# Explicit hand-out of six PSUM banks, and additions of the projection moved ahead of a step's first eviction

## The chip, the cores and the metric

The kernel runs on one core of a Trainium2 chip. The core has a matrix engine (TensorE, PE in the profile; its weight loads have a row of their own, PEld), a vector engine (VectorE, DVE), a scalar engine (ScalarE, ACT), GpSimd (POOL) and a queue that only issues transfers (SyncE, SP). Each engine works through its own list of instructions in order and waits on semaphores for the others. Results of TensorE go to PSUM, whose banks hold 128 partitions of 512 float32 values each, and VectorE and ScalarE read them from there.

The metric is device time in microseconds (us) of the whole program, lower is better. The time before is the median of three runs, 3659.57 us (3655.64 to 3660.37).

## The reference, cut to what matters

`x` has 16 samples of 256 channels on a 64 by 64 grid, all in float32. Two residual layers follow each other:

```python
x = x + conv(_gn(x))         # layer 0: group norm, then a grouped 3x3 convolution whose kernels are
                             # rotated per sample and group by angles computed from the pooled sample
x = x + attention(_gn(x))    # layer 1: group norm, then linear attention with 8 heads,
                             # a 5x5 depthwise convolution of the values, and a projection
...
q = relu(q) + 1e-6 ; k = relu(k) + 1e-6          # both over softplus(scale)
q = q ** 3 ; k = k ** 3                          # and rescaled to their norms of before
z = 1.0 / (einsum('bic,bc->bi', q, k.sum(axis=1)) + 1e-6)
kv_state = einsum('bjc,bjd->bcd', k, v)
out = einsum('bic,bcd->bid', q, kv_state) * z[..., None]
out = out + depthwise5x5(v)
out = out @ Wproj.T + bproj
```

## The kernel before, in words

A sample's 4096 positions are taken in 16 pairs of 128. For each sample `b` there is a key phase (`key_step`, positions by the pair: key and value products, the powers, and the sum of key times value that is kept in PSUM), a short passage (`between`) and an attention phase (`attention_step`, called with `p` = 1 to 17). Inside the `tc.manual_schedule()` of the main loop the order of instructions on each engine is the order of the calls in the code, so the calls of `attention_step` are to be read as a list of work for each engine.

An attention step works on three pairs at once, each at another stage. On TensorE the order is: `turn(b, p-1)` transposes the queries (tile `pt`, L698), `query_products(b, p+1)` makes the next queries (`pq`, L683), `turn_back(b, p-2)` transposes the attention output (`po`, L734), `attend(b, p-1)` multiplies with the key-value sum (`pn`, L715, in two PSUM banks of its own), `project(b, p-2)` makes the projection (`py`, L744). `add_up(b, p-3)` on VectorE adds the projection of the pair before to `x` in place (L756, two instructions), and `store` sends a finished quarter of the sample out once in four steps.

Into six of a sample's steps the convolution of the next sample is woven. `convolve(b+1, u, part)` comes last on TensorE in steps 2, 3, 4 (`u` = 0) and 9, 10, 11 (`u` = 1), with the parts A, P and B; it fills four tiles `pc` at once (L405), one for each `q` from 0 to 3. They are emptied in the step after, by `evict` with `q` = 0 to 3, spread over that step. A part A is emptied by ScalarE alone (L432). A part P is read twice: ScalarE writes it negated to one half of the rows (L428), then VectorE adds it to the other half (L434). A part B is added by VectorE (L430). I call a step by the part that it empties: an A step (p = 3 and 10), a P step (4 and 11), a B step (5 and 12). All but the last sample have a next one, so there are 15 samples with two P steps each, 30 in all.

All of these tiles but `pn` and the key-value sum, that is `pk`, `pt`, `pq`, `po`, `py`, `pd`, the four `pc` and some small ones, come from one PSUM pool of six places, `ps`, under one tag, "bank". A tile is asked for by `bank(name)`; which of the six places it gets is left to the framework, which takes one that is free as the program is laid out and makes the first matmul into it wait until the last reader of the tile before it is done. With four `pc` and one `py` held over the end of a step, a step that empties a convolution begins with one place free.

The lines that matter:

```python
        if part:
            evict(b + 1, u, part, 0)        # L864
        if p >= 3:
            add_up(b, p - 3)                # L866
            store(b, p - 3)
        if p - 1 < NP:
            turn(b, p - 1)                  # L870: asks for pt
            turned(b, p - 1)
        if part:
            evict(b + 1, u, part, 1)
        if p < NP:
            cube(f[p])
        if p + 1 < NP:
            query_products(b, p + 1)        # L877: asks for pq
```

Of the kernel before, what the change touches and what calls it, by code (L numbers as in the profile page):

```python
# [9 lines left out]
F32 = mybir.dt.float32  # L10
# [3 lines left out]
PSUM = bass.MemoryType.PSUM  # L14

P = 128
# [5 lines left out]
CH = 512  # L22
# [2 lines left out]
ROWS = CH // W  # L25


STRIP = 2 * ROWS
PAIRS = ROWS
LATE, LEAD = 3, 2  # L30
# [33 lines left out]
def conv_attention(ctx: ExitStack, tc: tile.TileContext, x, consts, kw, b1, w2, b2, b2r,  # L64
# [4 lines left out]
    def pool(name, bufs, **kw):  # L69
        return ctx.enter_context(tc.tile_pool(name=name, bufs=bufs, **kw))  # L70
# [7 lines left out]
    sp = pool("stats", 2)  # L78
    wtp = pool("wt", 1)
    dcp = pool("scratch1", 1, space=bass.MemoryType.DRAM)  # L80
    ps = pool("ps", 6, space=PSUM)
    psk = pool("psk", 1, space=PSUM)

    def const(name, shape, src=None):
# [2 lines left out]
            nc.sync.dma_start(t, src)  # L87
        return t

    def bank(name):  # L90
        return ps.tile([P, CH], F32, tag="bank", name=name)

    def halves(a):
        return a.rearrange("(t p) n -> p t n", p=P)
# [90 lines left out]
    def gn_coefs(st, b, which):  # L185


        mv = sp.tile([P, 2, 2], F32, tag="mv", name=f"mv{which}_{b}")
        for t in range(2):
            nc.vector.bn_aggr(mv[:, t, :], st[:, t])  # L190
        yield
        mean, var = mv[:, :, 0], mv[:, :, 1]
        co = sp.tile([P, 5, 2], F32, tag=f"co{which}", name=f"co{which}_{b}")
        a, pooled, d, v, m = (co[:, k, :] for k in range(5))
        pm = bank(f"pm{which}_{b}")[:, 0:2]
        nc.tensor.matmul(pm, lhsT=g8, rhs=mean, start=True, stop=True)
        nc.vector.tensor_copy(m, pm)
        nc.vector.tensor_sub(d, mean, m)
        nc.vector.tensor_mul(v, d, d)
        nc.vector.tensor_add(v, v, var)  # L200
        yield
        pv = bank(f"pv{which}_{b}")[:, 0:2]
        nc.tensor.matmul(pv, lhsT=g8, rhs=v, start=True, stop=True)
        vs = sp.tile([P, 2], F32, tag="vs", name=f"vs{which}_{b}")
        nc.vector.tensor_scalar(vs, pv, EPS_GN, None, ALU.add)
        nc.gpsimd.tensor_tensor(a, vs, mhalf, ALU.pow)
        yield
        if which == 0:
            nc.vector.tensor_mul(pooled, d, a)
        return a, pooled, m  # L210
# [7 lines left out]
    def prepare(b):  # L218
# [13 lines left out]
                                 start=t == 0, stop=t == 1)  # L232
        h = sp.tile([HID, 2], F32, tag="h", name=f"h_{b}")
        nc.vector.tensor_add(h, ph, b1_t)
        nc.vector.tensor_scalar(h, h, 0.0, None, ALU.max)
        yield
        pa = bank(f"pa_{b}")[:, 0:2 + 2 * HD]
# [10 lines left out]
        nc.vector.tensor_add(z, pa[:, 0:2], b2_t)  # L248
        mod = r_mod
        nc.vector.tensor_add(mod, pmod, b2r_t)  # L250

        nc.scalar.activation(mod, mod, AF.Tanh, scale=0.5)
        cs = sp.tile([P, 3, 2], F32, tag="cs", name=f"cs_{b}")
# [5 lines left out]
        pe = bank(f"pedge_{b}")[:, 0:NH]  # L259
        nc.tensor.matmul(pe, lhsT=sel, rhs=gm.rearrange("p t j -> p (t j)"), start=True, stop=True)  # L260
        nc.vector.tensor_copy(edge, pe)
        state[b]["edge"] = edge
        nc.vector.tensor_scalar(mod, mod, 0.5, 0.5, ALU.mult, ALU.add)
        yield
# [59 lines left out]
        def shifts(t):  # L324


            pb = bank(f"pbias_{b}_{t}")[:, 0:3]
            for j in range(4):
                for dx in range(3):
                    nc.tensor.matmul(pb[ts(j, HD), dx:dx + 1], lhsT=sums[t][:, dx, :], rhs=gm[:, t, j:j + 1],  # L330
                                     start=True, stop=True, tile_position=(0, HD * j))
            nc.vector.tensor_copy(shift[:, t, 0:3], pb)
            nc.vector.tensor_reduce(shift[:, t, 3:4], shift[:, t, 0:3], AX.X, ALU.add)
            nc.vector.tensor_scalar(shift[:, t, 3:4], shift[:, t, 3:4], -1.0, None, ALU.mult)

# [83 lines left out]
    def evict(b, u, part, q):  # L419

        at, shift = (2 * u + q // 2, q % 2), state[b]["shift"][:, q % 2, 3:4]
        pc = state[b]["pc"][q].rearrange("p (r w) -> p r w", w=W)
        fresh = at not in state[b]["x"]
        if fresh:
            state[b]["x"][at] = xp.tile([P, 2 * CH], F32, tag="x", name=f"x_{b}_{at[0]}_{at[1]}")
        rows = rows_16(b, u, q)
        if part == "P":
            nc.scalar.activation(rows[:, 1], pc, AF.Identity, bias=shift, scale=-1.0)  # L428
        if part == "B":
            nc.vector.tensor_add(rows[:, 1], pc, rows[:, 1])  # L430
        elif fresh:
            nc.scalar.activation(rows[:, 0], pc, AF.Identity, bias=shift)  # L432
        else:
            nc.vector.tensor_add(rows[:, 0], pc, rows[:, 0])  # L434

    def settle(b, u, s, q):

# [28 lines left out]
    for name, src, bsrc in (("kv", wkv, brow[C:3 * C]), ("q", wq, brow[0:C])):  # L466
        n = src.shape[1]
# [27 lines left out]
    for (w, br), lo in zip(wl.values(), (0, 2 * C)):  # L495
# [3 lines left out]
        n = w.shape[2]  # L499
# [3 lines left out]
    pb = bank("pb")[:, 0:2]  # L503
    for co in range(2):
        for t in range(2):
            nc.tensor.matmul(pb[:, co:co + 1], lhsT=wp_t[:, t, ts(co, P)], rhs=dwb_t[:, t:t + 1],
                             start=t == 0, stop=t == 1)
    nc.vector.tensor_add(bp_t, bp_t, pb)


    vpad = [dcp.tile([BC, H + 4, NJ, C], F32, tag=f"vpad{n}", name=f"vpad{n}") for n in range(2)]
# [21 lines left out]
    def fold_shift(b, name):  # L533
        w, br = state[b][name]
        n = br.shape[1]
        pb = bank(f"pb{name}_{b}")
        for t in range(2):
            nc.tensor.matmul(pb[:, 0:n], lhsT=state[b]["gn1"][1][:, t:t + 1].to_broadcast([P, P]), rhs=w[:, t, :],
                             start=t == 0, stop=t == 1)
        nc.vector.tensor_sub(br, br, pb[:, 0:n])  # L540

    def norm1(b):
        a, _, m = yield from gn_coefs(state[b]["st1"], b, 1)
# [11 lines left out]
    def relu(r, pm, bias):  # L555

        nc.vector.tensor_add(pm, pm, bias)  # L557
        nc.vector.tensor_tensor(r, pm, eps_t.unsqueeze(1).to_broadcast(r.shape), ALU.max)
# [33 lines left out]
    def key_bias(b, n, j):  # L592
        _, br = state[b]["kv"]
        f = state[b]["k"][n]
        pm = f["pm"][j]
        relu(f["r"][:, j:j + 1, :], pm[:, 0:C].unsqueeze(1), br[:, 0:C].unsqueeze(1))
        nc.vector.tensor_add(vbuf[n % NV][:, j, 0:HD, :].rearrange("p c h -> p (c h)"), pm[:, C:2 * C], br[:, C:2 * C])

    def key_store(b, n):
        for j in range(2):  # L600
# [47 lines left out]
    def depthwise(b, half, c):  # L648


        if c == 0:
            state[b]["fm"] = fmp.tile([P, 16, C], F32, tag="fm", name=f"fm_{b}_{half}")
        fm = state[b]["fm"]
        vb = vh[0:KP].rearrange("p R (m j) (c h) -> p R m j c h", j=4, h=NH)
        pd = bank(f"pd_{b}_{half}_{c}").rearrange("p (k n) -> p k n", k=4)
        for k in range(4):
            for j in range(4):
                nc.tensor.matmul(  # L658
                    pd[ts(j, HD), k, :].rearrange("p (R m h) -> p R m h", R=4, m=4),
                    lhsT=band_t[:, c + k, :],  # L660
                    rhs=vb[:, :, :, j, c + k, :],
                    start=True, stop=True,
                    tile_position=(0, HD * j),
                )
        nc.scalar.copy(fm[:, :, c * NH:(c + 4) * NH].rearrange("p T (k h) -> p k T h", k=4),
                       pd.rearrange("p k (T h) -> p k T h", h=NH))


    def blocked(b, m):
# [19 lines left out]
    def query_bias(b, m):  # L689
        f = state[b]["f"][m]  # L690
        relu(f["r"], f["pq"], state[b]["q"][1].unsqueeze(1).to_broadcast([P, 2, C]))

    def turn(b, m):

# [6 lines left out]
    def turned(b, m):  # L701
        qT = op.tile([P, 2, 2, P], F32, tag="qT", name=f"qT_{b}_{m}", bufs=1)
        nc.scalar.copy(qT, state[b]["pt"])  # L703
        state[b]["qT"] = qT

    def attend(b, m):
# [22 lines left out]
    def turn_back(b, m):  # L729

        po = bank(f"po_{b}_{m}").rearrange("p (t j n) -> p t j n", t=2, j=2)
        for j in range(2):
            for t in range(2):
                nc.tensor.transpose(po[:, t, j, :], state[b]["o"][j][:, ts(t, P)], ident)  # L734
        oT = op.tile([P, 2, 2 * P], F32, tag="oT", name=f"oT_{b}_{m}", bufs=1)
        nc.scalar.copy(oT.rearrange("p t (j n) -> p t j n", j=2), po)  # L736
        state[b]["oT"] = oT

    def project(b, m):
# [12 lines left out]
    def add_up(b, m):  # L752
        i, R = divmod(m, 2)
        for co in range(2):
            xt = chunk(b, i, co).rearrange("p (y R n) -> p R y n", y=BR, R=2)[:, R]
            nc.vector.scalar_tensor_tensor(xt, state[b]["py"][:, co], bp_t[:, co:co + 1], xt, ALU.add, ALU.add)  # L756

    def store(b, m):
        I, R = divmod(m, 4)
        if R == 3:  # L760
            for t in range(2):
                nc.sync.dma_start(out[b, ts(t, P), ts(I, 2 * CH)], state[b]["x"].pop((I, t)))
# [89 lines left out]
    def attention_step(b, p, chain):  # L852
# [4 lines left out]
        f = state[b]["f"]  # L857
        n = p - NP - 2 + LEAD if more else -1
        u, part = PARTS.get(p - 1, (None, None)) if more else (None, None)
        v, s, early, late = SETTLES.get(p, (0, 0, (), ())) if more else (0, 0, (), ())  # L860
        if p - 1 < NP:
            ratio(f[p - 1], True)
            root(f[p - 1])
        if part:  # L864
            evict(b + 1, u, part, 0)
        if p >= 3:  # L866
            add_up(b, p - 3)
            store(b, p - 3)
        if p - 1 < NP:
            turn(b, p - 1)  # L870
            turned(b, p - 1)
# [13 lines left out]
        if n >= 0:  # L885
            k = state[b + 1]["k"]
# [179 lines left out]
```

## Time and profile before

| what | value |
|---|---|
| median of three runs | 3659.57 us |
| the profiled execution's own time | 3660.74 us |
| its span, from the first to the last instruction | 3659.0 us |
| mean granted TensorE clock | 0.994 of full speed |
| busy: VectorE, ScalarE, GpSimd | 2541.2, 2034.6 and 1980.4 us (69, 56 and 54% of the span) |
| projection added to x (L756) | 512 instructions, 474 ns median |
| part P added by VectorE (L434) | 120 instructions in the woven steps, 681 ns median |
| part P written by ScalarE, part A likewise (L428, L432) | 0.69 us each |
| part B and part A convolution (L405), start to start of the next `pt` | 6.51 and 6.46 us |

The profile is one execution. Its span is 1.7 us shorter than that execution's own time, which is 1.2 us above the median. A row of the timeline gives start and duration in us, engine, line, operation, and in brackets how long the engine was idle before it and which instruction ended that idle time. A row of the table of waits gives who waited, for whom, and then the sum in us, the number of times and the longest.

### The profile page before, as it was taken

The numbers are of one execution on the slowest core, as the hardware profiler recorded it, in microseconds if no ns is written. First come the engines' busy times: TensorE is split into PE (matmuls) and PEld (weight loads), VectorE is DVE, ScalarE is ACT, GpSimd is POOL, SyncE is SP. The second block draws the span as 40 slices with busy tenths as digits, with TensorE's granted clock in tenths as the row PEclk, the third lists the DMA queues.
The fourth block names the chain that finished last, engine by engine and source line by source line (L and its number), as shares of the span: only waits on it lengthen the run. The fifth ranks groups of instructions, "written<-read, shape, count | busy, mean of one in ns | idle before, by whom it ended". The sixth has DMA issues, their size and how long they took to land. (4 is left out here: it accounts for less than half of the span.)

```text
span 3659.0 us, 109568 instructions
## 1 busy us (share of the span) xinstructions
PE 3425.6 (94%) x43496; PEld 2563.6 (70%) x43496; DVE 2541.2 (69%) x6883; ACT 2034.6 (56%) x6501; POOL 1980.4 (54%) x2298
## 2 busy tenths in 40 slices
PE   2899999999999999999999999999999999999999
PEld 1467777776777767776677777777777677767778
DVE  4667768676686767767677686776866677676656
ACT  2365655647556465654656556475564646546565
POOL 4255555556555465554655555565554655546545
PEclk9899999999999999999999999999999999999999
DMA  4353552625436253452635526354362534525242
GB/s 134 110 180 106 161 159 86 197 87 184 140 115 190 83 189 111 150 172 72 203 106 161 158 87 193 91 185 139 113 191 84 186 114 148 168 77 181 78 145 99
DMA packets 191172, 505.90 MB, mean 138 GB/s; under 512 B 30741, under 2 KB 103959, under 8 KB 178372
## 3 DMA queue, kind: packets, MB, share of 16 engines
q1 hardware_dynamic: 190660, 498.89, 42.8%
q8 instruction: 344, 5.64, 0.6%
q14 instruction: 168, 1.38, 0.1%
HBM read 363.24 MB, written 135.53 MB: 136 GB/s over the span
## 5 line engine op out<-in xcount | busy, mean ns | idle before, releaser
L588 PE MATMUL pk<-wkv,x 128*128 128x512 f32 x2048 | 951.5, 611 | 0.0
L726 POOL TENSOR_TENSOR o<-o,fm 128x256 f32<-128x256 f32 x512 | 364.8, 733 | 918.9 <-DVE o L724 704.7
L588 PEld LDWEIGHTS pk<-wkv,x 128*128 128x128 f32 x2048 | 617.6, 310 | 213.6 <-issue 6.5
L683 PE MATMUL pq<-wq,xq 128*128 128x256 f32 x2048 | 492.2, 383 | 21.7 <-DVE x L434 11.5
L744 PE MATMUL py<-oT,wp 128*128 128x256 f32 x2048 | 505.7, 390 | 0.8 <-ACT oT L736 0.7
L564 ACT ACTIVATE r_k<-rk 128x256 f32<-128x256 f32 x1024 | 416.3, 407 | 152.9 <-POOL rk L567 92.6
L564 ACT ACTIVATE r_q<-rq 128x256 f32<-128x256 f32 x1024 | 413.5, 408 | 138.5 <-POOL rq L567 135.9
L683 PEld LDWEIGHTS pq<-wq,xq 128*128 128x128 f32 x2048 | 369.9, 191 | 72.1 <-DVE x L434 15.3
L736 ACT COPY oT<-po 128x512 f32<-128x512 f32 x256 | 150.1, 586 | 469.5 <-PE po L734 469.1
L744 PEld LDWEIGHTS py<-oT,wp 128*128 128x128 f32 x2048 | 369.2, 189 | 51.4 <-issue 3.6
L567 POOL TENSOR_TENSOR rk<-r_k,rk 128x512 f32<-128x512 f32 x256 | 327.0, 1277 | 96.7 <-ACT r_k L564 94.1
L576 POOL TENSOR_TENSOR s_k<-s_k,phalf 128x2 f32<-128x2 f32 x256 | 176.8, 691 | 356.9 <-DVE s_k L573 345.5
L557 DVE TENSOR_TENSOR pq<-pq,bq 128x512 f32<-128x512 f32 x256 | 177.4, 693 | 272.7 <-PE pq L683 230.6
L608 ACT ACTIVATE rk<-rk,s_k 128x256 f32<-128x256 f32 x512 | 231.4, 499 | 213.7 <-POOL s_k L576 213.7
L567 POOL TENSOR_TENSOR rq<-r_q,rq 128x512 f32<-128x512 f32 x256 | 327.2, 1278 | 0.0
L384 POOL TENSOR_TENSOR arena<-arena 128x512 f32<-128x512 f32 x244 | 303.8, 1279 | 7.1 <-PE pc_0B L405 3.7
L557 DVE TENSOR_TENSOR pk<-pk,bkv 128x256 f32<-128x256 f32 x512 | 218.0, 426 | 121.7 <-PE pk L588 119.9
L703 ACT COPY qT<-pt 128x512 f32<-128x512 f32 x256 | 148.7, 581 | 261.9 <-PE pt L698 260.2
L715 PE MATMUL pn<-kvx,qT 128*128 128x132 f32 x2048 | 274.0, 277 | 0.0
L576 POOL TENSOR_TENSOR s_q<-s_q,phalf 128x2 f32<-128x2 f32 x256 | 179.3, 700 | 144.1 <-DVE s_q L573 140.4
L715 PEld LDWEIGHTS pn<-kvx,qT 128*128 128x128 f32 x2048 | 250.5, 190 | 3.7 <-ACT qT L703 3.1
L658 PE MATMUL pd<-vh,band 107*32 107x128 f32 x8192 | 236.3, 274 | 6.5 <-issue 4.5
(161 smaller groups left out, 5974.1 us busy)
## 6 DMA issues: line engine op xcount, KB each, us to landing
vh<-vpad SPq DMA_DIRECT2D x256, 384.0 KB
vh<-vpad SPq DMA_DIRECT2D x256, 360.0 KB
vpad<-arena SPq DMA_DIRECT2D x512, 128.0 KB
out<-x SPq DMA_DIRECT2D x128, 512.0 KB
xs<-in_x SPq DMA_DIRECT2D x224, 256.0 KB
arena<-in_x SPq DMA_DIRECT2D x248, 144.0 KB
arena<-in_x SPq DMA_DIRECT2D x248, 136.0 KB
xs<-in_x SPq DMA_DIRECT2D x16, 512.0 KB
```

Source lines behind the costliest of these rows:

```text
L384: nc.gpsimd.tensor_add(s[:, j], g[:, j, odd:odd + STRIP:2], g[:, j, even:even + STRIP - 1:2])
L557: nc.vector.tensor_add(pm, pm, bias)
L564: nc.scalar.activation(f["r2"][:, j, :], f["r"][:, j, :], AF.Square, accum_out=f["s"][:, k, j:j + 1])
L567: nc.gpsimd.tensor_mul(f["r"], f["r2"], f["r"])
L576: nc.gpsimd.tensor_tensor(f["s"][:, 3, :], f["s"][:, 2, :], phalf, ALU.pow)
L588: nc.tensor.matmul(pm, lhsT=chunk(b, n // 2, t)[:, T % BC:CH:BC], rhs=w[:, t, :], start=t == 0, stop=t == 1)
L608: nc.scalar.mul(f["r"][:, j, :], f["r"][:, j, :], f["s"][:, 3, j:j + 1])
L658: nc.tensor.matmul(pd[ts(j, HD), k, :].rearrange("p (R m h) -> p R m h", R=4, m=4), lhsT=band_t[:, c + k, :], rhs=vb[:, :, :, j, c + k, :] ...
L683: nc.tensor.matmul(pq[:, j, :], lhsT=xq[:, t, ts(j, P)], rhs=w[:, t, :], start=t == 0, stop=t == 1)
L715: nc.tensor.matmul(pn[:, :, 4 * hh:4 * hh + 4], lhsT=qT[:, hh, j, :], rhs=kvx[:, hh], start=True, stop=True)
L726: nc.gpsimd.tensor_add(o, o, fm[:, 2 * (m % NCH) + j, :])
L744: nc.tensor.matmul(py[:, co].rearrange("p y (J c) -> p J y c", c=BC), lhsT=wp_t[:, t, ts(co, P)], rhs=oT[:, t, :].rearrange("p (J y c) -> ...
```

## The change

It does two things. The pool of six interchangeable places becomes six tags with one place each, `bank0` to `bank5`. A list `idle` in the code holds the names of the free ones; `bank(name)` takes the first of the list, and a new call `leave(name)`, put in the code behind the last reader of each tile, appends its place to the end. So the order of the calls in the code decides which place a tile gets. And in `attention_step` the lines `add_up` and `store` come before `evict(…, 0)` and no longer after it.

```diff
+BANKS = 6
...
-    ps = pool("ps", 6, space=PSUM)
+    ps = pool("ps", 1, space=PSUM)
...
+    idle, held = [f"bank{k}" for k in range(BANKS)], {}
+
     def bank(name):
-        return ps.tile([P, CH], F32, tag="bank", name=name)
+        held[name] = idle.pop(0)
+        return ps.tile([P, CH], F32, tag=held[name], name=name)
+
+    def leave(name):
+        idle.append(held.pop(name))
...
         else:
             nc.vector.tensor_add(rows[:, 0], pc, rows[:, 0])
+        leave(f"pc_{b}_{u}{part}_{q}")
...
         relu(f["r"], f["pq"], state[b]["q"][1].unsqueeze(1).to_broadcast([P, 2, C]))
+        leave(f"pq_{b}_{m}")
...
         nc.scalar.copy(qT, state[b]["pt"])
+        leave(f"pt_{b}_{m}")
...
         nc.scalar.copy(oT.rearrange("p t (j n) -> p t j n", j=2), po)
+        leave(f"po_{b}_{m}")
...
             nc.vector.scalar_tensor_tensor(xt, state[b]["py"][:, co], bp_t[:, co:co + 1], xt, ALU.add, ALU.add)
+        leave(f"py_{b}_{m}")
...
-        if part:
-            evict(b + 1, u, part, 0)
         if p >= 3:
             add_up(b, p - 3)
             store(b, p - 3)
+        if part:
+            evict(b + 1, u, part, 0)
         if p - 1 < NP:
             turn(b, p - 1)
             turned(b, p - 1)
```

The other tiles of the pool (`pk`, `pd` and the small ones of the norms and the rotation) get a `leave` behind their last reader in the same way. No instruction is added or removed.

More of the change, by code (lines that the diff above doesn't have):

```diff
@@ L197, in gn_coefs @@
         nc.vector.tensor_copy(m, pm)
+        leave(f"pm{which}_{b}")
         nc.vector.tensor_sub(d, mean, m)
@@ L205, in gn_coefs @@
         nc.vector.tensor_scalar(vs, pv, EPS_GN, None, ALU.add)
+        leave(f"pv{which}_{b}")
         nc.gpsimd.tensor_tensor(a, vs, mhalf, ALU.pow)
@@ L234, in prepare @@
         nc.vector.tensor_add(h, ph, b1_t)
+        leave(f"ph_{b}")
         nc.vector.tensor_scalar(h, h, 0.0, None, ALU.max)
@@ L250, in prepare @@
         nc.vector.tensor_add(mod, pmod, b2r_t)
+        leave(f"pa_{b}")
         nc.scalar.activation(mod, mod, AF.Tanh, scale=0.5)
@@ L261, in prepare @@
         nc.vector.tensor_copy(edge, pe)
+        leave(f"pedge_{b}")
         state[b]["edge"] = edge
@@ L332, in shifts @@
             nc.vector.tensor_copy(shift[:, t, 0:3], pb)
+            leave(f"pbias_{b}_{t}")
             nc.vector.tensor_reduce(shift[:, t, 3:4], shift[:, t, 0:3], AX.X, ALU.add)
@@ L508, in conv_attention @@
     nc.vector.tensor_add(bp_t, bp_t, pb)
+    leave("pb")
     vpad = [dcp.tile([BC, H + 4, NJ, C], F32, tag=f"vpad{n}", name=f"vpad{n}") for n in range(2)]
@@ L540, in fold_shift @@
         nc.vector.tensor_sub(br, br, pb[:, 0:n])
+        leave(f"pb{name}_{b}")
     def norm1(b):
@@ L597, in key_bias @@
         nc.vector.tensor_add(vbuf[n % NV][:, j, 0:HD, :].rearrange("p c h -> p (c h)"), pm[:, C:2 * C], br[:, C:2 * C])
+        leave(f"pk_{b}_{2 * n + j}")
     def key_store(b, n):
@@ L666, in depthwise @@
                        pd.rearrange("p k (T h) -> p k T h", h=NH))
+        leave(f"pd_{b}_{half}_{c}")
     def blocked(b, m):
```

## The prediction
> **What bounds the kernel now.** I read the page first, then the waits of TensorE, then the timeline of single steps. The page says that TensorE (PE) is nearly always busy:
>
> ```profile
> span 3659.0 us, 109568 instructions
> ...
> PE 3425.6 (94%) x43496; PEld 2563.6 (70%) x43496; DVE 2541.2 (69%) x6883; ACT 2034.6 (56%) x6501; POOL 1980.4 (54%) x2298
> ```
>
> That leaves 3659.0 - 3425.6 = 233 us of idle TensorE, the only time that a change of order can win. The table of waits, TensorE only, splits it. Of the rows that recur in every sample these matter:
>
> ```profile
> PE po L734 <- POOL o L726: 57.8, 148, 1.1
> ...
> PE pq L683 <- DVE x L434: 11.5, 16, 0.7
> PE pq L683 <- ACT qT L703: 10.2, 14, 0.7
> ```
>
> Large single waits (16.5, 16.0, 15.4, 14.7 us) lie before the main loop and stay. The first row is data: the transpose waits for the attention output. The other two are odd, since the query products `pq` need neither the convolution's rows (L434) nor the turned queries (L703). They can only wait for the place in PSUM. 16 + 14 = 30 is the number of P steps, and going through the timeline I find the wait in every P step and in no other. One P step in full:
>
> ```profile
> 993.15 0.69 ACT L428 ACTIVATE x<-pc_1P,shift 128x512 f32<-128x512 f32 x1 [2.41 <-PE pc_1P L405]
> 993.24 0.66 PE L698 MATMUL pt<-consts,rq 128*128 128x128 f32 x4
> 993.87 0.69 DVE L434 TENSOR_TENSOR x<-pc_1P,x 128x512 f32<-128x512 f32 x1 [1.83 <-ACT x L428]
> 993.99 0.59 ACT L703 COPY qT<-pt 128x512 f32<-128x512 f32 x1 [0.15 <-PE pt L698]
> 994.48 0.86 DVE L756 SCALAR_TENSOR_TENSOR x<-py,bp,x 128x256 f32<-128x256 f32 x2
> 994.62 1.99 PE L683 MATMUL pq<-wq,xq 128*128 128x256 f32 x8 [0.72 <-DVE x L434]
> 995.26 0.68 DVE L434 TENSOR_TENSOR x<-pc_1P,x 128x512 f32<-128x512 f32 x1
> 996.45 0.60 PE L734 MATMUL po<-consts,o 128*128 128x128 f32 x4
> 996.65 0.70 DVE L557 TENSOR_TENSOR pq<-pq,bq 128x512 f32<-128x512 f32 x1 [0.70 <-PE pq L683]
> ```
>
> `pt` ends at 993.90, `pq` starts at 994.62, just behind the end of the first L434 (993.87 + 0.69 = 994.56). That L434 is late because ScalarE reads the same bank first, and ScalarE had to wait for the convolution's end. VectorE idled 1.83 us before it, while the additions of the projection (L756), ready for a whole step, stood behind it in its queue. The A step just before shows the order without the wait:
>
> ```profile
> 984.46 0.66 PE L698 MATMUL pt<-consts,rq 128*128 128x128 f32 x4
> 984.95 1.89 PE L683 MATMUL pq<-wq,xq 128*128 128x256 f32 x8
> 986.47 0.57 PEld L734 LDWEIGHTS po<-consts,o 128*128 128x128 f32 x4
> 986.68 0.60 PE L734 MATMUL po<-consts,o 128*128 128x128 f32 x4
> ```
>
> From `pt` to `po` is 2.22 us there and 3.21 us in the P step.
>
> **The queue of places, by hand.** Call the one free place at a step's start X, the projection's Y, the convolution's c0 to c3. Before: evict 0 frees c0, then the addition frees Y, so longest-free first is X, c0, Y: `pt` takes X, `pq` takes c0, `po` takes Y. That the framework hands out this way is a reading, but it fits: taking the latest freed place, `pt` would have waited for L756 until 995.34, and it started at 993.24. The other row, L703, would mean that `pq` took X from `pt`; but in the P steps that I compared both releasers end within 0.03 us of each other, and in A steps `pq` starts before L703 does. After: X, Y, c0. `pt` takes X, `pq` takes Y, `po` takes c0. The next convolution takes c1, `pq`'s place, c2 and `po`'s place, by the same releases as before.
>
> **The change part by part.** *The additions first.* L756 (0.86 us for two) runs in VectorE's gap: its work before ends at 992.04 (L573, from 990.89, 1.15 us long), so they end near 992.9, before `pt` ends. Cost: nothing, covered by the 1.83 us of idle time; without that cover a P step would pay 0.86 us, 30 x 0.86 = 26 us. In B steps VectorE idles 1.41 us at the same point, and 0.83 us before L557 anyway, so nothing is won or lost there; in A steps evict 0 is ScalarE's, and VectorE's order doesn't change. No transfer changes its order on SP: an eviction issues none, and the store waits for the same L756.
>
> *The wait.* With Y free at 992.9, `pq` can follow `pt` at 0.49 us as in the A step. `po` then needs c0, free at 994.56; it would come at 993.24 + 2.22 = 995.46, so it doesn't wait. `pn` needs the turned queries of 994.58 and would come at 995.9. Per P step TensorE wins between 0.72 us (the idle time alone) and 3.21 - 2.22 = 0.99 us (start to start).
>
> *What is late next.* The B convolution at the step's end. Its third bank is c2, released by the L434 that starts at 999.62 and ends at 1000.29, 0.59 us behind the convolution's start at 999.70; the weight loads idle 0.45 us there, and the whole part takes 6.51 us against 6.46 for A, so that 0.05 us is lost today. VectorE's chain to this L434 runs from L557, which waited 0.70 us for `pq`. Now it is held by the second L434: ScalarE's second L428 ends at 994.47 + 0.69 = 995.16, so that L434 ends near 995.87, and L557 starts near 995.80 (engines overlap neighbours by 0.07) in place of 996.65: 0.85 us earlier, where the convolution is 0.99 us earlier. The bank comes 0.14 us later, relative to its matmuls. I take all of this as lost: 0.99 - 0.14 = 0.85 us per P step, the value inside the two bounds that the rows of the step give.
>
> *The place by tag.* The price in other steps is nothing where the first place of the list has long been left. I followed the list through a plain step (five free, four asked for, each left a step earlier), the key steps (one held at a time, six in turn), and the depthwise group of p = 9, the tightest: its sixth tile gets `pq`'s place, left at 970.81 by L558, and is due near 967.55 + 5 x 0.87 = 971.9. All have cover; the last has 1.1 us.
>
> *Sum.* 30 x 0.85 = 25.5 us; 3660.74 - 25.5 = 3635.2 against this execution, 3659.57 - 25.5 = 3634.1 against the median, which I predict. Bounds: 30 x 0.72 = 21.6 gives 3638.0, 30 x 0.99 = 29.7 gives 3629.9.
>
> **A rule weighed against it.** The rows first: in the P step the weight loads of `pq` begin only at 994.61, after 0.96 us without any. The Trainium skill, page "TensorE: Matmul & The Clock Gate", section "Architectural detail: the array is 16× 32×32, not 1× 128×128", says that the engine's queue can pull weight loads ahead of matmuls in flight. By that rule the loads would be done during the wait, only the matmul's 0.72 us would be lost, and the sum would be 21.6 us. By the rows, where load and matmul start together, it is the larger one.
>
> The page "Perfetto Trace Analysis", section "Identifying the Most-Contended Engine", calls matmul busy time no good measure of how close TensorE is to its limit. That speaks against taking the 94% for a bound; the sum above rests on starts of matmuls alone, and by the page it would be the same.
>
> **The rivals.** *The time goes to the next wait (no change).* If the L434 behind the B convolution's third bank kept its time, the bank would come 0.59 + 0.99 us after the start and give all back: 3659.6. For it: that wait exists (17 times 0.5 us on PEld for each half). Against: VectorE's chain there waits on `pq` itself. Chance 0.07. *It doesn't do what it says:* if places were handed out otherwise than I read, `pq` may have waited for something else that stays: 3659.6 again. Against: the list in the code is explicit now. 0.03.
>
> *Slower.* In the A steps of p = 10 the evictions of q = 0 and 1 ask for new tiles in SBUF, and the store now comes ahead of them. If they got the places that this very store is emptying, ScalarE would stand in evict 0 until the transfer has landed, with the turned queries behind it in its queue, `pn` behind those, and TensorE behind `pn`. The store is issued at 979.47, evict 0 is due at 983.97, and the transfers' share falls from 0.95 to 0.05 at 983.5, so it would cost about nothing. From 25.5 / 15 = 1.7 us per sample it eats the gain, from 2.2 us (another 7.3 / 15) it makes the kernel slower. With a landing 3 us late: 15 x 3 - 25.5 = +19.5, 3679. Chance 0.07.
>
> **How the numbers follow.** What a measurement of this kernel can tell from no change is about 0.2%, 7.3 us. Forecast (21.6 to 29.7 us won): 0.78. No change: 0.10, from both rivals. Slower: 0.07, of which 0.01 is within 7.3 us. The rest, 0.05, is a gain smaller than the bounds, when part of the saved time meets the POOL waits of the later steps; I count 0.04 of it faster. So faster 0.82, same 0.12, slower 0.06. The range goes from the lower bound less the runs' spread below the median (3.9 us, so 3626) up to 3643, which takes in the upper bound and the smaller gains.
>
> **What would show it.** Right: no wait of `pq` for L434 or L703 in the table; L756 ahead of L434 in P steps; `pt` to `po` 2.2 us; `po` without a new wait for L434; B convolutions a little longer than 6.51 us. Wrong: a wait of like size at `po` or at the convolution, ScalarE idle before L432 on a transfer, or new waits at `pd`.

## The result, and the profile after

The changed kernel is slower, by little: the median of seven runs is 3668.19 us (3664.05 to 3672.96), beside 3656.75 us (3653.52 to 3661.78) for seven runs of the kernel before. The ratio is 1.0030, with a 95% interval of 1.0019 to 1.0041. The forecast of 3634 us lies 34 us below that, and its range ended at 3643.

The first lines of the page of the kernel after, and two rows of its table of waits, TensorE only (sum in us, number of times, the longest):

```profile
span 3671.2 us, 109727 instructions
...
PE 3459.1 (94%) x43496; PEld 2559.5 (70%) x43496; DVE 2549.8 (69%) x6883; ACT 2034.4 (55%) x6501; POOL 1981.6 (54%) x2298
```

```profile
PE po L754 <- POOL o L746: 56.6, 144, 0.8
...
PE pd L675 <- DVE x L777: 4.1, 5, 2.5
```

Both rows of `pq` are gone, with their 30 waits, and no wait of `po` has come in their place. By the difference of the two busy numbers TensorE would idle 212 us now, 21 us less than before, and yet the span is 12.2 us longer. So the time must be inside the groups of matmuls that count as busy. The table of groups, TensorE only, says where (matmuls x number, busy us, mean ns of one, idle before). First before, then after:

```profile
L405 PE MATMUL pc_1B<-arena,wt 32*32 32x504 f32 (+1 forms) x3072 | 106.5, 593 | 0.0
...
L405 PE MATMUL pc_0B<-arena,wt 32*32 32x504 f32 (+1 forms) x2976 | 105.6, 600 | 1.1 <-DVE x L434 1.1
```

```profile
L418 PE MATMUL pc_0B<-arena,wt 32*32 32x504 f32 (+1 forms) x2976 | 121.3, 606 | 21.4 <-DVE x L447 10.9 <-ACT x L445 9.6 <-issue 0.4
L418 PE MATMUL pc_1B<-arena,wt 32*32 32x504 f32 (+1 forms) x3072 | 120.0, 593 | 0.7
```

The B convolutions issue as many matmuls of nearly the same mean length as before, but the group is 13.5 and 15.7 us longer. (The idle time of 10.9 and 9.6 us is nearly all two single waits ahead of the main loop.) A matmul of such a group lasts 0.59 us and overlaps the ones behind it, so a pause of about that length between two starts leaves hardly any idle time in this row, and a higher busy number can be a wait. The row of the weight loads shows the wait itself. The timeline of one P step after, the counterpart of the one in the prediction:

```profile
991.05 1.15 DVE L589 TENSOR_TENSOR s_q<-s_q 128x2 f32<-128x2 f32 x1
...
992.13 0.86 DVE L777 SCALAR_TENSOR_TENSOR x<-py,bp,x 128x256 f32<-128x256 f32 x2
...
993.41 0.66 PE L717 MATMUL pt<-consts,rq 128*128 128x128 f32 x4
...
993.90 1.89 PE L701 MATMUL pq<-wq,xq 128*128 128x256 f32 x8
994.04 0.69 DVE L447 TENSOR_TENSOR x<-pc_1P,x 128x512 f32<-128x512 f32 x1 [1.05 <-ACT x L441]
...
995.37 0.69 DVE L447 TENSOR_TENSOR x<-pc_1P,x 128x512 f32<-128x512 f32 x1 [0.64 <-ACT x L441]
...
995.63 0.60 PE L754 MATMUL po<-consts,o 128*128 128x128 f32 x4
...
996.49 1.30 POOL L583 TENSOR_TENSOR rq<-r_q,rq 128x512 f32<-128x512 f32 x1
...
997.30 0.53 DVE L457 TENSOR_TENSOR x<-x,shift 128x16 f32<-128x16 f32 x1
...
998.88 7.52 PE L418 MATMUL pc_1B<-arena,wt 32*32 32x512 f32 x192
...
999.29 1.27 DVE L447 TENSOR_TENSOR x<-pc_1P,x 128x512 f32<-128x512 f32 x2
...
1000.02 0.24 PEld L418 LDWEIGHTS pc_1B<-arena,wt 32*32 32x32 f32 x32 [0.95 <-DVE x L447]
...
1006.34 0.66 PE L717 MATMUL pt<-consts,rq 128*128 128x128 f32 x4
```

The first half is what was forecast: the additions (now L777) run ahead of the eviction, `pq` follows `pt` at 0.49 us, and `pt` to `po` is 2.22 us. Then the convolution starts, issues the 16 weight loads of two banks, and stands until 1000.02. Its third bank is released by the first of the two L447 at 999.29, which ends near 999.97: 1.09 us behind the start. Start to start of the next `pt` is now 7.46 us. The same stretch before, in the lines that the prediction didn't show:

```profile
996.33 1.28 POOL L567 TENSOR_TENSOR rq<-r_q,rq 128x512 f32<-128x512 f32 x1
...
997.99 0.18 DVE L443 TENSOR_TENSOR x<-x,shift 128x16 f32<-128x16 f32 x1
...
999.62 1.27 DVE L434 TENSOR_TENSOR x<-pc_1P,x 128x512 f32<-128x512 f32 x2
999.70 0.21 PEld L405 LDWEIGHTS pc_1B<-arena,wt 32*32 32x32 f32 x24 [0.33 <-issue]
999.70 6.58 PE L405 MATMUL pc_1B<-arena,wt 32*32 32x512 f32 x192
1000.35 0.72 PEld L405 LDWEIGHTS pc_1B<-arena,wt 32*32 32x32 f32 x33 [0.45 <-DVE x L434]
```

Two things differ. The weight loads stop after 24, three banks, and not after 16, two: the late bank was the **fourth** before and is the **third** now. And the small addition at the rows' edges, L443, takes 0.18 us here and 0.53 us as L457 after, where it ends together with GpSimd's L583 (996.49 + 1.30 = 997.79).

Which bank each tile has is written in the programs as built. The table says whose place a tile takes over in the P steps of this kernel and of the experiments below (`pt` is the one of the same step):

```
                   pq takes   po takes   B convolution takes, in order
                   the place of          q = 0, 1, 2, 3
before, u = 0      pt         c0         c1, po, pq, c2
before, u = 1      c0         py         c1, po, pq, c2
after              py         c0         c1, pq, c2, po
e1                 c0         py         c1, pq, c2, po
e2, u = 0          pt         py         c1, po, pq, c2
e2, u = 1          py         c0         c1, po, pq, c2
e3, e4, e5         py         c0         c1, pq, po, c2
e6                 as after
e8                 as before
```

The rows u = 0 of before and e2 hold for 14 of 15 samples. In one `pq` stands in another place (c0 in before, `py` in e2), which is why the table of waits before has 16 waits for L434 and 14 for L703.

The depthwise matmuls (`pd`, in the passage and at p = 9) are the second place where the kernels differ. Their busy and idle time was 236.3 + 6.5 = 242.8 us before. After, by this row, it is 241.8 + 13.6 = 255.4:

```profile
L675 PE MATMUL pd<-vh,band 107*32 107x128 f32 x8192 | 241.8, 276 | 13.6 <-issue 4.9 <-DVE x L777 4.1 <-DMA arena<-in_x 2.4
```

Summing from start to start of groups of matmuls over the whole trace, between the profiled executions (3672.96 - 3660.74 = 12.2 us):

| where | us |
|---|---|
| `pt` to `po` in the 30 P steps | -29.7 |
| B convolutions, start to next `pt` (195.2 to 224.2) | +29.0 |
| depthwise, behind the first `pt` (226.8 to 238.4) | +11.6 |
| A convolutions: u = 0 from 124.6 to 128.8, u = 1 from 99.6 to 97.9 | +2.5 |
| everything ahead of the first `pt` (235.1 to 233.2) | -2.0 |

These add up to 11.4 us; the other groups together make up the remaining 0.8.

About 5.1 us of the depthwise row is the clock. In three of these groups of the kernel after the granted clock was 0.82, 0.85 and 0.81 (2007.0 to 2016.3, 2307.0 to 2318.5 and 3127.5 to 3136.7 us), and in each the clock record holds one stretch of 3.4 us at half speed. By these numbers the loss is an estimate of 0.18 x 9.3 + 0.15 x 11.5 + 0.19 x 9.2 = 5.1 us. The kernel before has no such stretch between 231 and 3656 us. One of the three lies just behind a wait of TensorE for the addition of the projection (2.5 us), the two others behind waits for transfers (1.8 and 1.0 us).

### The profile page after: what moved, and what is told of

Same layout as the page of the kernel before. It is cut to its first block, busy times and chain, and to the rows that moved or that the text cites. A ratio compares the mean times of both kernels' runs of the same rounds, so it can differ in the third digit from the quotient of the medians.

```text
span 3671.2 us, 109727 instructions
## 1 busy us (share of the span) xinstructions
PE 3459.1 (94%) x43496; PEld 2559.5 (70%) x43496; DVE 2549.8 (69%) x6883; ACT 2034.4 (55%) x6501; POOL 1981.6 (54%) x2298
## 5 line engine op out<-in xcount | busy, mean ns | idle before, releaser
L583 POOL TENSOR_TENSOR rk<-r_k,rk 128x512 f32<-128x512 f32 x256 | 327.3, 1278 | 96.9 <-ACT r_k L580 94.3
L573 DVE TENSOR_TENSOR pq<-pq,bq 128x512 f32<-128x512 f32 x256 | 177.0, 691 | 286.1 <-PE pq L701 286.0
L583 POOL TENSOR_TENSOR rq<-r_q,rq 128x512 f32<-128x512 f32 x256 | 327.8, 1280 | 0.0
L573 DVE TENSOR_TENSOR pk<-pk,bkv 128x256 f32<-128x256 f32 x512 | 217.9, 426 | 121.2 <-PE pk L604 120.6
L675 PE MATMUL pd<-vh,band 107*32 107x128 f32 x8192 | 241.8, 276 | 13.6 <-issue 4.9
```

Source lines behind the costliest of these rows:

```text
L583: nc.gpsimd.tensor_mul(f["r"], f["r2"], f["r"])
L675: nc.tensor.matmul(pd[ts(j, HD), k, :].rearrange("p (R m h) -> p R m h", R=4, m=4), lhsT=band_t[:, c + k, :], rhs=vb[:, :, :, j, c + k, :] ...
```

## The experiments

The theory to be tested: the gain at `pq` is there, but the new order of places hands it back at the B convolution and at the depthwise group. Rivals: the order of the calls does the harm, or the wait moves whatever is done.

### One half of the change at a time

e1 keeps the explicit places and puts eviction 0 back ahead of the additions:

```diff
+        if part:
+            evict(b + 1, u, part, 0)
         if p >= 3:
             add_up(b, p - 3)
             store(b, p - 3)
-        if part:
-            evict(b + 1, u, part, 0)
```

> The change without its second part: explicit places, but the first eviction again ahead of the additions. Theory (order of the places in the B convolution: c2, which VectorE empties last, stands third and no longer fourth, and a late third place costs all of its delay while a late fourth one costs nearly nothing): pq waits 0.72 us in each P step as before, the B convolution starts as late as before and still loses about 0.45 us to c2, 6.9 to 7.0 us against 6.51; 3657 + 30 x 0.45 + some 10 us of waits in the depthwise group = 3677 to 3688 us. Rival (c2 is simply freed later relative to the start, whichever place it has): here c2 is no later than before, so the B convolution takes 6.51 us and the time is 3655 to 3668 us.

Measured: 3683.93 us, ratio 1.0067 (1.0051 to 1.0084), as the theory expected and slower than the whole change. All 30 waits of `pq` are back, and there is the depthwise wait; from its table of waits:

```profile
PE pq L701 <- DVE x L447: 21.5, 30, 0.7
PE pd L675 <- DVE x L777: 7.4, 6, 3.0
```

With `pq` late as before, its B convolution still takes 6.97 us, where the kernel before takes 6.51. The third bank is 0.59 us behind the start in e1, as the fourth one was before. So the same lateness costs 0.5 us at the third place and 0.05 at the fourth.

e2 is the other half: the pool of six interchangeable places of the kernel before, and only the additions ahead of eviction 0.

> The change without its first part: one pool of six interchangeable places as before, additions ahead of the first eviction. The framework then hands pq the projection's place and leaves c2 the fourth of the B convolution. Theory (place order): no wait of pq, B convolution 6.5 to 6.65 us, 3657 less 25 to 30 = 3627 to 3632 us. Rival (c2 too late at any place, about 1.1 us behind the start): B convolution 7.0 to 7.45 us, 3640 to 3657 us.

Measured: 3653.91 us, ratio 0.9981 (0.9971 to 0.9990). This is a small gain, and the expectation missed by over 20 us. Its waits of `pq` say why:

```profile
PE pq L683 <- ACT qT L703: 10.2, 14, 0.7
```

The row for L703 stayed as it was. In 14 of the 15 steps with u = 0 the framework gives `pq` the place of `pt`, before and in e2, and that place is free only when the turned queries have been copied out. The order of the additions can't touch it. In the other 16 steps 0.98 us is won, and the B convolution goes from 6.51 to 6.99 us, though the late bank stays its fourth: 16 x (0.98 - 0.48) = 8.0 us against 6.0 measured. There the bank is 1.08 us late, and the rival's lower end (7.0 us) is what is seen.

### The third place against the fourth

e3 is the kernel after with the place of c2 put on the list behind that of `po`, so that the B convolution has it fourth:

```diff
-        leave(f"pc_{b}_{u}{part}_{q}")
+        if q != 2 or b == 0:
+            leave(f"pc_{b}_{u}{part}_{q}")
...
+            leave(f"pc_{b + 1}_{u}{part}_2")
             evict(b + 1, u, part, 3)
```

> The change whole, with one line moved: the place of the third tile of a convolution goes back to the list behind the attention transpose of its step, not at its own eviction, so that c2 stands fourth in the B convolution. Theory (place order): B convolution 6.5 to 6.65 us, no wait of pq, 3668 less 25 to 29 = 3638 to 3643 us; the waits of the depthwise group stay. Rival (lateness at any place): B convolution 7.0 to 7.45 us, 3653 to 3668 us.

Measured: 3653.25 us, ratio 0.9982 (0.9969 to 0.9994), with the B convolution at 6.99 us. That is the lower end of the rival's range, and 15 us less than the median of the kernel after (17.5 us by the two ratios, since the two were measured in different series), where the theory wanted 25 to 29. Two lines of its P step:

```profile
998.07 0.20 PEld L418 LDWEIGHTS pc_1B<-arena,wt 32*32 32x32 f32 x24 [0.33 <-issue]
...
999.21 0.24 PEld L418 LDWEIGHTS pc_1B<-arena,wt 32*32 32x32 f32 x32 [0.93 <-DVE x L447]
```

The loads of three banks go out and then wait for L447 all the same. The fourth place buys about half a microsecond, and a bank that is 1.09 us late needs more. So the place was one cause; that VectorE empties c2 too late is another.

### The depthwise group

By the programs as built the depthwise tiles of p = 9 went around four places before, and after around six, of which the fourth tile gets `py`'s and the sixth `pq`'s, both left in that very step. In a sample where VectorE is late, after:

```profile
2307.11 2.83 PE L675 MATMUL pd<-vh,band 107*32 107x128 f32 x96
2307.44 1.30 DVE L125 BATCH_NORM_STATS2 st<-xs 128x6 f32<-128x512 f32 x2 [2.91 <-DMA xs<-in_x]
2308.91 2.60 DVE L589 TENSOR_TENSOR s_q<-s_q 128x2 f32<-128x2 f32 x1
2311.44 0.86 DVE L777 SCALAR_TENSOR_TENSOR x<-py,bp,x 128x256 f32<-128x256 f32 x2
2312.45 6.04 PE L675 MATMUL pd<-vh,band 107*32 107x128 f32 x160 [2.50 <-DVE x L777]
```

96 matmuls are three tiles of 32. The fourth waits 2.50 us for the addition, which stands behind statistics that waited 2.91 us for a transfer. e4 adds to e3 that in this step the places of `py` and `pq` come back on the list only behind the group:

```diff
+    kept, keep = [], [False]
...
-        idle.append(held.pop(name))
+        (kept if keep[0] else idle).append(held.pop(name))
...
+        keep[0] = p == SECOND
         if p >= 3:
             add_up(b, p - 3)
             store(b, p - 3)
+        keep[0] = False
...
+        keep[0] = p == SECOND
         if p + 1 < NP:
             query_products(b, p + 1)
             query_bias(b, p + 1)
+        keep[0] = False
...
         if p == SECOND:
             for c in range(0, HD, 4):
                 depthwise(b, 1, c)
+            idle.extend(kept)
+            kept.clear()
```

> As the run before, and in the step of the second depthwise group the places of the projection and of the queries go back to the list behind that group. If the other 10 us that the change lost come from depthwise tiles that wait for the projection's place (VectorE's additions stand behind statistics that wait for a transfer), the group goes back to 7.15 to 7.2 us and the time is 6 to 11 us under the run before, 3627 to 3637 us. If they come from elsewhere, it equals the run before.

Measured: 3649.39 us, ratio 0.9967 (0.9954 to 0.9979). The group's row in the table shows no wait for the addition any more:

```profile
L678 PE MATMUL pd<-vh,band 107*32 107x128 f32 x8192 | 236.2, 273 | 7.7 <-issue 6.1 <-DMA vpad<-arena 0.4 <-DMA arena<-in_x 0.3
```

236.2 + 7.7 = 243.9 us is about the 242.8 of the kernel before. That these waits come from the place is shown. The size is less sure: the expectation was 6 to 11 us under e3, the medians differ by 3.9 us, and their intervals overlap. (The trace of e3 is no measure of the difference. Its execution of 3661.46 us is the second slowest of nine, with four stretches at half the clock; e4 has none.) In the kernel after the group lost 12.6 us, of which 4.1 are waits for the addition, 5.1 by the estimate above the clock, and the rest waits for transfers and the like.

Over all traces, busy and idle time of the depthwise matmuls together is 245.4 to 260.7 us in the five kernels in which they can get the places of `py` and `pq` of their step (after, e1, e3, e6, e7), and 240.1 to 244.7 us in the five others. So the loss goes with the places, but e7, at 245.4 us, hardly has it. Why the waits for transfers and the stretches of lower clock come mostly with these places is not shown.

### Emptying the late bank earlier

In the code eviction 2 stands behind the two early `settle` calls, each an L457 and statistics (L458) of 0.69 us. e5 adds to e4 that it comes ahead of them:

```diff
         if p + 1 < NP:
             query_products(b, p + 1)
             query_bias(b, p + 1)
+        if part:
+            evict(b + 1, u, part, 2)
         for q in early:
             settle(b + 1, v, s, q)
...
-        if part:
-            evict(b + 1, u, part, 2)
```

> As the run with the depthwise places, and the eviction of the third tile (q = 2) moved ahead of the two early settles in VectorE's order, so that c2 is free some 0.9 us before the B convolution starts and not 1.1 us after it. Theory now (the late release of c2 costs what it exceeds, about 0.1 us of grace for the third place and 0.55 us for the fourth; 6.99 us measured for 1.1 us late in fourth place): B convolution 6.45 to 6.5 us, 30 x 0.5 = 15 us less than that run's 3649, 3630 to 3638 us. Rival (the convolution itself runs into something else when it starts earlier, the sums or the queries' place): 6.8 to 7.0 us, 3645 to 3650 us.

Measured: 3631.88 us, ratio 0.9923 (0.9910 to 0.9937), as expected, and faster than both kernels. It is 29.2 us under the kernel before of its series (3661.10 us), about the 29.7 us that the change wins at `pq`. The P step of e5:

```profile
988.80 1.30 POOL L586 TENSOR_TENSOR rq<-r_q,rq 128x512 f32<-128x512 f32 x1
...
989.61 0.68 DVE L449 TENSOR_TENSOR x<-pc_1P,x 128x512 f32<-128x512 f32 x1
990.21 0.18 DVE L460 TENSOR_TENSOR x<-x,shift 128x16 f32<-128x16 f32 x1
...
991.19 0.23 PEld L420 LDWEIGHTS pc_1B<-arena,wt 32*32 32x32 f32 x32 [0.33 <-issue]
991.19 6.52 PE L420 MATMUL pc_1B<-arena,wt 32*32 32x512 f32 x192
```

The addition that empties c2 (L449) now ends at 990.29, 0.90 us ahead of the convolution's start. The loads of all four banks, 32, go out without a wait, and the B convolution takes 6.45 us, as little as the undisturbed A. Besides, L460 starts just as GpSimd's multiplication ends (990.10) and takes 0.18 us again.

e6 makes only this one move in the kernel after, with the places as the change has them.

> The change whole, with that same one move and nothing else: c2 stays the third place of the B convolution. Theory (only lateness counts; the order of places matters no more once c2 is free in time): B convolution 6.45 to 6.5 us against the change's 7.45, 30 x 0.97 = 29 us less than the change's 3668, 3636 to 3643 us. Rival (the third place has a price of its own): 6.9 us, about 3652 us.

Measured: 3643.37 us, ratio 0.9954 (0.9941 to 0.9968), at the edge of what was expected. The B convolution takes 6.46 us with c2 third: a bank that is free in time costs nothing at the third place, as it costs nothing at the fourth in e5. The depthwise group keeps its loss (238.5 + 13.8 = 252.3 us), 7.6 us more than e5 has (237.7 + 7.0), of the 11.5 us between their medians.

e8 makes the same move in the kernel before, with its pool and its order of calls.

> The kernel before, with the one move of the best run alone: the eviction of the third tile ahead of the early settles; pool and additions as before. Theory (before, the wait of pq hid the late c2, and only both moves together gain): pq waits 0.72 us in each P step, the B convolution goes from 6.51 to 6.46 us, 30 x 0.05 = 1.5 us, 3654 to 3660 us, no change. Rival (that move is worth its 29 us by itself): 3630 to 3640 us.

Measured: 3661.88 us, ratio 0.9995 (0.9986 to 1.0004): no change, with the B convolution at 6.46 us and `pt` to `po` at 3.20 to 3.22. The move alone wins nothing, since there the wait was 0.05 us. It pays only together with the change, which makes the bank late.

### Is it the second input of the small addition?

In the kernel after, L457 takes 168 to 186 ns in 195 instances without GpSimd beside it, and in the 61 others it ends 39 to 49 ns behind the end of a running GpSimd instruction (60 times the multiplication L583). Both its inputs are in SBUF. e7 replaces it, in the kernel after, by a form with one input tensor:

```diff
-        nc.vector.tensor_add(e, e, shift[:, t, 0:3:2].unsqueeze(1).to_broadcast([P, PAIRS, 2]))
+        for k in range(2):
+            nc.vector.tensor_scalar(e[:, :, k], e[:, :, k], shift[:, t, 2 * k:2 * k + 1], None, ALU.add)
```

> The change whole, with the edge addition of each settle (one tensor-plus-tensor of 128x16, both inputs in SBUF) written as two instructions of 128x8 that add a per-partition scalar. In the change's trace that addition takes 0.53 us in the P step instead of 0.17, and ends 0.04 us behind a GpSimd operation of 1.3 us that runs beside it (61 of 61 times where one runs). Theory (VectorE's second tensor input from SBUF has to wait for GpSimd, and this is why c2 came 0.5 us earlier and not 0.85): the form with one tensor input doesn't wait; four of them take 0.4 to 0.7 us where the two took 0.70, c2 comes 0.1 to 0.3 us earlier, B convolution 7.15 to 7.35 us against 7.45, 3 to 9 us less than the change's 3668. Rival (the addition waits for something else, the eviction just before or the queries' bias): the first of them takes as long, B convolution 7.45 to 7.6 us, 3668 to 3673 us.

Measured: 3701.59 us, ratio 1.0099 (1.0085 to 1.0113), outside both expectations. From its P step:

```profile
1004.49 1.30 POOL L584 TENSOR_TENSOR rq<-r_q,rq 128x512 f32<-128x512 f32 x1
...
1005.30 0.65 DVE L458 TENSOR_SCALAR x<-x,shift 128x8 f32<-128x8 f32 x2
...
1006.60 0.35 DVE L458 TENSOR_SCALAR x<-x,shift 128x8 f32<-128x8 f32 x2
1006.88 0.18 PEld L418 LDWEIGHTS pc_1B<-arena,wt 32*32 32x32 f32 x16 [0.33 <-issue]
...
1008.33 0.24 PEld L418 LDWEIGHTS pc_1B<-arena,wt 32*32 32x32 f32 x32 [1.26 <-DVE x L447]
```

The pair still takes 0.65 us beside L584 and 0.35 alone, twice the 0.17 of the one instruction it replaces; elsewhere a single one took up to 1.31 us beside GpSimd. In 62 cases the instruction that met a GpSimd one ended 30 to 42 ns behind it, just as L457 does. The chain to L447 got longer, the bank came 1.39 us behind the start, and the B convolution took 7.76 us. So the experiment made the chain longer where it was meant to make it shorter. The theory that the form with one input doesn't wait for GpSimd falls, so a second input tensor is not needed for the wait; what it takes is open. The B convolutions are only 30 x 0.31 = 9 us of what e7 loses against the kernel after. TensorE's waits for the attention output before `po` grew by another 19.5 us, from 56.6 to 76.1, and were not followed further. What the run does give is a third size of lateness:

| third or fourth bank late by | loss at the third place | at the fourth |
|---|---|---|
| free ahead of the start | 0 (e6, 6.46) | 0 (e5, 6.45) |
| 0.59 us | 0.5 (e1, 6.97) | 0.05 (before, 6.51) |
| 1.09 us | 1.0 (after, 7.45) | 0.5 (e3, 6.99) |
| 1.39 us | 1.3 (e7, 7.76) | not measured |

The loss is each B convolution's median less the 6.46 us of the A convolution. It is the lateness less about 0.1 us at the third place, and less about 0.55 us at the fourth.

## Why the prediction was wrong, point by point

**The gain** was there. In all 30 P steps the wait of `pq` went, the additions cost nothing in VectorE's gap, `po` didn't wait for c0, and `pt` to `po` fell by the upper bound: 29.7 us by the sums of starts.

**"The next convolution takes c1, pq's place, c2 and po's place, by the same releases as before"** is the step that failed, and with it the 0.14 us that the prediction takes off per step. The order after was read rightly from the code. The order before was never read from the built program, only inferred from one timeline, and it was c1, `po`, `pq`, c2. So the change moves c2, the latest of the four, from the fourth place to the third. The timeline in the prediction's own hands spoke of it: 24 weight loads ahead of the wait are three banks of eight, so the late one was the fourth. After, `po`'s place stands behind c2 on the list since its `leave` is called later; in time it is free earlier, as `po` is copied out at 996.91 (ScalarE, in the step shown) and c2 at 999.97. The list is longest-free first in the order of the code, not in the order of time. e1 and e3 show the effect from both sides. In place of 0.14 us the B convolution lost 7.45 - 6.51 = 0.94 us per step: about 0.46 by the place (e1, 6.97) and 0.48 by the lateness (e3, 6.99).

**Before was not longest-free first either.** The prediction took the row of 14 waits for L703 as an uncertain attribution. It was literal: for u = 0 `pq` stood in `pt`'s own place. This didn't cost the forecast anything, as the change ends that wait too, but it made the expectation of e2 miss.

**"What is late next"** was sized wrongly. The bank was to come 0.14 us later relative to its matmuls; it comes 0.50 us later (1.09 instead of 0.59). VectorE's chain did start earlier, the query bias by the 0.85 us forecast (2.56 us behind the start of `pt` instead of 3.41), but the first L457 then meets GpSimd's multiplication, which before had just ended, and takes 0.53 us instead of 0.18. With 0.35 us lost there the arithmetic closes: 0.14 + 0.35 = 0.49. With c2 in the fourth place this alone leaves e3, at 3653 us.

**"The place by tag"** had the right step and the wrong tile. I followed the sixth depthwise tile, to `pq`'s place, in a sample where VectorE was on time. The fourth, in `py`'s place, waits for the addition five times, up to 2.5 us, and in the step shown its cover was taken away by a late transfer. The prediction put this term at nothing. The whole group lost 12.6 us, of which 4.1 are these waits and about 5.1 the clock, and in e4 it is within 1.1 us of before.

**The rivals.** The one called "the time goes to the next wait" named the right place, L434 behind the B convolution's third bank, at a chance of 0.07 and with a full give-back as its worst case. Its condition, that VectorE's chain wouldn't move, didn't hold; the chain moved, and the bank's place in the convolution made up the rest. Two of the three signs that were named for being wrong are in the trace: a wait of like size at the convolution, and new waits at `pd`. The slower rival, a store's places in SBUF, didn't happen, so that the kernel got slower for another reason than the one that was given a chance: in ScalarE's table of waits the evictions of part A at p = 10 wait for the convolution alone, 15 times, 85.9 us in all, before and after. What stretches single A convolutions of u = 0 (their sum varies from 124.6 to 129.5 us over the kernels here, with medians of 8.26 to 8.28) stays open. It isn't the clock, which in the kernel after was at full speed in all of them.

**The rules weighed.** In this case the starts of matmuls were the measure that held: 0.98 us won per step and not the 0.72 us of the wait alone, and busy time rose by 33.5 us with the same matmuls. That the small addition waits for GpSimd agrees with what the Trainium skill says on the page "SBUF — State Buffer", section "Who interferes with whom": a VectorE instruction with two inputs in SBUF contends with a GpSimd instruction that reads SBUF. The rows here are the 0.53 us beside L583 and the 0.17 us without; the rule was not used in the prediction, where it would have spoken against moving the chain earlier. This sentence of the page doesn't cover e7, whose form has one input tensor and was lengthened too.

## What to carry to other kernels

When a tile changes its place, look up which place every tile after it gets, before and after, from the built program and not from a rule about the pool; a place that comes free late belongs to the last tile of a group, or must be emptied earlier. A wait taken off one engine makes the work behind it on other engines start earlier, and what that work now meets has to be looked up again for each instruction up to the next release. And where TensorE's busy time rises with the same matmuls, look at the idle time of its weight loads, where a wait shows, and at the granted clock of that stretch.

## What the runs showed of the hardware

In these kernels a convolution that fills four banks at once absorbed a late fourth bank up to about 0.55 us and a late third one up to about 0.1 us, and beyond that lost the whole rest (the table above, from three sizes of lateness). A VectorE addition of 128x16 elements, 0.17 us alone, ended 39 to 49 ns behind the running GpSimd instruction in 61 of 61 cases, while in the same trace the query bias (L573) and the projection's additions (L777), which have a PSUM source, kept their lengths beside GpSimd (medians 427 beside and 433 ns alone, 472 and 475). So did the statistics (L458), with one input, in the only two cases there are (666 and 677 ns, median 694 alone). Splitting that addition in two of 128x8 elements by a scalar made it longer, about 0.23 us each alone, and 62 of them ended 30 to 42 ns behind a GpSimd instruction.

The granted clock fell to half in eleven stretches between 250 us and the end of the last sample, over all ten traces: three in after, three in e1, four in e3 and one in e6. Each lasted 3.4 us, one of them 6.8. In the 3.4 us ahead of each, TensorE had been idle for 1.5 to 3.0 us in sum, and ten of the eleven lie at depthwise groups. Not every such wait is followed by one: e2 idles 2.4 us of 3.4 at 2661 to 2665 us without it. The wait of 1.4 us that recurs once per sample never is. What decides is not shown.
